# Four conv layers on one core: the planner's freedom on POOL, the queue of the first weights, and the blocks of five weight steps

## The chip, the cores and the metric

The kernel runs on one core of a Trainium2 chip. The metric is the time of one execution in microseconds (us) on the device. The engines are TensorE (PE for the matmuls, PEld for its weight loads), VectorE (DVE), ScalarE (ACT), GpSimd (POOL) and SyncE (SP, which here only starts DMAs). Each runs its own instructions in order and waits for the others by semaphores.

## The reference, cut to what matters

Four layers on x of shape (16, 256, 28, 28). The change lies in what the first layer does and in the weights that the third one needs:

```python
# layer 0
out = sign(x)
scaling = mean(abs(weights), axis=(1, 2, 3))
y = conv3x3(out, sign(weights)) * scaling
yn = (y - mean(y)) * rsqrt(var(y) + EPS)      # over batch and image
x = yn * gamma + beta + x
# layer 1: 3x3 conv of sign(x), gates, 1x1 conv of a sign, residuals
# layer 2: two 3x3 convs of signs with sign(w1), sign(w2), each scaled by mean(abs(w))
# layer 3: attention over the 784 pixels of each image
```

## The kernel before, in words

256 channels are two halves of 128 partitions. A layer with signs on both sides (layer 0 and the two convs of layer 2) is made by `sign_layer` (L273). It packs the weights of two output channels into one number (`dst = 4095 * sign + sign`, L235), so that one matmul makes both halves of the output, and takes them apart again with a rounding trick (`apart`, L298: ACT L302 and L303, DVE L304).

The work goes in 33 blocks of half an image, 392 columns; the last half image is two blocks of 196 (`BLOCKS`, L47). A block is 18 matmuls (`products`, L283; L292): six weight chunks by three taps, into one of three PSUM accumulators (`conv_ps`, L370). Blocks 0 and 1 are made together, chunk by chunk (`together=2`), since at the start the chunks arrive one after the other.

The loop over blocks j (L318 to L333) is written out by hand, in this order: matmuls of block j; ACT's signs of the next image (L398) if j is even; `post` of block j - 1 (statistics on DVE, L532, and for the lower half of an image its store on POOL, L534); at j = 27 `gather` (L153: a memset on POOL, two aggregations on DVE, L157, and L158); `late`, what the last block's step left over; one step; `apart` of block j.

A **step** is a piece of side work, one in each block from j = 2 on; `None` in the list of steps leaves a block without one. In layer 0 (L518 to L527) the list holds seven steps that prepare layer 1's weights (`w1_step`, `fw_step`, here steps 0 to 6), six that prepare the first packed weights of layer 2 (`signs2` and `sums2`, steps 7 to 12), the six sums of layer 0's own absolute weights (`sums_`), and `constants` (L485), which zeroes the two `pad` tiles on POOL (L487), copies to POOL's `doubts`, works out small constants on DVE and starts eight small DMAs. Each of steps 7 to 12 does, through `both` and `sign_weights` (L220): ACT's sign of a 384 KB chunk into tile `sg` (L234; one buffer), DVE's reduction of its absolute values (L246) and the add to the total (L124); left over for the next block is DVE's pack of `sg` (L235), and after the last step `total_up` (L251), four small matmuls on PE (L254) that add the total over partitions. The load of step n + 2 is started on SP after the work of step n (`load_ahead`, L214), into a tile of three buffers.

Who orders the instructions: within `tc.manual_schedule(engines=...)` (L316) those of the named engines that are made in it keep the order of the program among themselves; here PE, ACT, DVE and SP. Everything else is put in order by a planner, which may bring an instruction forward, also into or ahead of such a part. So the memsets of `pad` (L487), made in block 21, ran at 3.89 us.

At the start (L413 to L429) SP starts the DMAs of the first weight chunk, of the first image's two halves, of the other five chunks, and of images 1 and 2; ACT takes the sign of each chunk when it lands. `keep_busy` (L375) gives PE idle matmuls to keep its clock up where it would pause: eight at the start, thirty after layer 0. After layer 0 the statistics are finished (`norm`, L177), image 0 is normalized (`enter`, L587), and layer 1 starts.

Of the kernel before, what the change touches and what calls it, by code (L numbers as in the profile page):

```python
# [35 lines left out]
ET = mybir.EngineType  # L36
# [43 lines left out]
def forward(ctx: ExitStack, tc: tile.TileContext, d: dict, out: bass.AP, careful: bool):  # L80
# [3 lines left out]
    nc = tc.nc  # L84
# [27 lines left out]
    CHUNKS = [(k, g) for g in range(3) for k in range(2)]  # L112
# [10 lines left out]
    def tt(o, a, b, op):  # L123
        V.tensor_tensor(o, a, b, op)  # L124
        return o
# [70 lines left out]
        return r, tt(c, beta, c, ALU.subtract)  # L196


    def load_taps(pool, src, k, g, tag="st", bufs=2):
        st = pool.tile([P, 3, 256], F32, tag=tag, name="st", bufs=bufs)  # L200
        nc.sync.dma_start(out=st, in_=src[k, :, 3 * g:3 * g + 3, :])
        return st

    def packed_weights(pool, **kw):
# [9 lines left out]
    def load_ahead(steps, n, now=True):  # L214

        for s in steps[:n] if now else ():
            s.load()
        return [lambda s=s, t=t: (s.work(), t.load() if t else None)[0] for s, t in zip(steps, steps[n:] + [None] * n)]

    def sign_weights(pool, dst, src, total, acc, stage=("st", 2), tmp=None, ab_tag="rn", sg=("sg", 1)):  # L220


        sts, all_ = {}, []
        tmp = tmp or pool

        def load(k, g):
            if (k, g) not in sts:
                sts[k, g] = load_taps(pool, src, k, g, *stage)

        def sign(k, g):  # L230
            st = sts[k, g]
            n = CHUNKS.index((k, g))
            t = tmp.tile([P, 3, 256], BF16, tag=sg[0], name="sg", bufs=sg[1])
            A.activation(t, st, AF.Sign, saturate=False)  # L234
            return lambda: V.scalar_tensor_tensor(  # L235
                dst[:, n], t[:, :, P:], PACK, t[:, :, 0:P], ALU.mult, ALU.add
            )

        def add_up(k, g):
            st = sts.pop((k, g))  # L240
            if not all_:
                all_.append(tmp.tile([P, 256], F32, tag="total", name="sums", bufs=1))
                ab = all_[0]
            else:
                ab = tmp.tile([P, 256], F32, tag=ab_tag, name="ab", bufs=2)
            V.tensor_reduce(ab, st.rearrange("p t o -> p o t"), AX.X, ALU.add, apply_absolute_value=True)  # L246
            if ab is not all_[0]:
                tt(all_[0], all_[0], ab, ALU.add)
            return total_up if (k, g) == CHUNKS[-1] else lambda: None

        def total_up():  # L251
            part = acc.tile([P, 2], F32, tag="sm", name="sumabs")
            for mo in range(2):
                T.matmul(part[:, mo:mo + 1], lhsT=all_[0][:, mo * P:(mo + 1) * P], rhs=ones, start=True, stop=True)  # L254
            V.tensor_scalar(total, part, 1.0 / K9, None, ALU.mult)

        return [[Step(lambda c=c: load(*c), lambda c=c, f=f: f(*c)) for c in CHUNKS] for f in (sign, add_up)]

    def both(first, second):
        def work(f, s):  # L260
            rest = f.work(), s.work()
            return lambda: [r() for r in rest]

        return [Step(f.load, lambda f=f, s=s: work(f, s)) for f, s in zip(first, second)]
# [8 lines left out]
    def sign_layer(pads, w, temp, room, sign, post, steps, moments, together=1):  # L273

        pss = [None] * NB
        abs_ = [None] * NB

        groups = 2 if careful else 1  # L280
        size = 6 // groups

        def products(*js):  # L283
            for j in js:
                pss[j] = conv_ps()
            for n, (k, g) in enumerate(CHUNKS):
                for j in js:
                    i, r0, rows = BLOCKS[j]
                    for t in range(3):
                        r, c = divmod(3 * g + t, 3)  # L290
                        r += r0
                        T.matmul(  # L292
                            pss[j][:, n // size, :rows * S].rearrange("p (a b) -> p a b", b=S), lhsT=w[:, n, t, :],
                            rhs=pads[:, i % 2, k, r:r + rows, c:c + S],
                            start=(n % size == 0 and t == 0), stop=(n % size == size - 1 and t == 2),
                        )

        def apart(j):  # L298
            for g in range(groups):
                n = BLOCKS[j][2] * S  # L300
                t, ab, ps = temp("t1")[:, :n], room(j, g), pss[j][:, g, :n]
                A.activation(t, ps, AF.Identity, bias=rounding, scale=1.0 / PACK)  # L302
                A.activation(ab[:, 1], t, AF.Identity, bias=unrounding)  # L303
                V.scalar_tensor_tensor(ab[:, 0], ab[:, 1], -PACK, ps, ALU.mult, ALU.add)  # L304
                if g == 0:
                    abs_[j] = ab
                else:
                    tt(abs_[j], abs_[j], ab, ALU.add)

        def sign_image(i):  # L310

            for r0, r1 in ((0, HR + 1), (HR + 1, S)) if i < together else ((0, S),):
                sign(i, slice(r0, r1), lambda k: inner(pads[:, i % 2], k, r0, r1))

        late = None
        with tc.manual_schedule(engines={ET.PE, ET.Activation, ET.DVE, ET.SP}):  # L316
            sign_image(0)
            for j in range(NB):  # L318
                if j == 0:
                    products(*range(together))  # L320
                elif together <= j:
                    products(j)
                if j % 2 == 0 and j // 2 + 1 < B:
                    sign_image(j // 2 + 1)
                if j > 0:
                    post(j - 1, abs_[j - 1])
                if j == EARLY + 1:
                    moments.gather()
                if late:
                    late()  # L330
                step = steps.pop(0) if j >= 2 and steps else None
                late = step() if step else None
                apart(j)  # L333
            post(NB - 1, abs_[NB - 1])
        assert not steps and not late

    def inner(pad, k, r0=0, r1=S):
        return pad[:, k, 1 + r0:1 + r1, 1:S + 1]
# [28 lines left out]
    with tc.tile_pool(name="ps_conv", bufs=3, space=PSUM) as psc, \  # L367
            tc.tile_pool(name="ps_sm", bufs=2, space=PSUM) as pss:

        def conv_ps():  # L370
            return psc.tile([P, 2, 512], F32, tag="cv", name="cv")
# [9 lines left out]
        with tc.tile_pool(name="ph1", bufs=1) as ph:  # L381
# [4 lines left out]
            def load_x(b, integers=False, rows=((0, S),)):  # L386
                if not xs[b]:
                    xs[b] = ph.tile([P, 2, N], F32, tag="xs", name=f"xs{b}", bufs=4)
                for r0, r1 in rows:
                    n = slice(r0 * S, r1 * S)  # L390
                    nc.sync.dma_start(out=xs[b][:, :, n], in_=d["x"][b][:, :, n])
                if integers:
                    ns[b] = ph.tile([P, 2, N], F32, tag="n", name=f"n{b}", bufs=2)
                    nc.sync.dma_start(out=ns[b], in_=n0d[b])
# [7 lines left out]
            def temp(tag):  # L402
                return ph.tile([P, HN], F32, tag=tag, name=tag, bufs=2)
# [9 lines left out]
            signs, sums_ = sign_weights(ph, w0, d["w0"], sf0, pss, ("yu", 6), sg=("t1", 2))  # L413
# [2 lines left out]
            keep_busy(8)  # L416

            top, bottom = ((0, HR + 1),), ((HR + 1, S),)
            signs[0].load()
            load_x(0, rows=top)  # L420
            load_x(0, rows=bottom)
            for step in signs[1:]:
# [39 lines left out]
            def fw_step():  # L462
                sts = []

                def load():
                    sts.append(xpool.tile([P, 3, 256], F32, tag="x2", name="stf", bufs=3))
                    nc.sync.dma_start(out=sts[0][:, 0:2, :], in_=d["fw"])

                return Step(load, lambda: split2(fw, sts[0][:, 0:2, :]))
# [48 lines left out]
            steps = [w1_step(k, c) for k in range(2) for c in range(3)] + [fw_step()]  # L518
            w2a = packed_weights(wpool, tag="wa2")
            signs2, sums2 = sign_weights(xpool, w2a, d["w2a"], sf1, pss, ("x2", 3), tmp=ph)  # L520
            steps = load_ahead(steps + both(signs2, sums2), 2)
# [1 line left out]
            for i, x in enumerate(sums_):  # L523
                steps[3 * i + 1:3 * i + 1] = [x.work, None]
            steps[19:19] = [constants, None]
            steps[-5:-5] = [None]
            steps[-2:-2] = [None]  # L527

            def post0(j, ab):
                b, r0, rows = BLOCKS[j]  # L530
# [4 lines left out]

            mom = block_moments("l0")
            sign_layer(fpads, w0, temp, room0, sign0, post0, steps, mom, together=2)
            for b in range(2):
                xs[b] = None
# [327 lines left out]
            with tc.manual_schedule(engines={ET.PE, ET.DVE, ET.Activation}):  # L867
# [23 lines left out]
                g = gates(hidden_b(B, hidden_a(B, px)))  # L891
# [41 lines left out]
                g = gates(h)[:, 1]  # L933
# [27 lines left out]
        with tc.tile_pool(name="ph2", bufs=1) as ph:  # L961
# [56 lines left out]
            steps = both(*sign_weights(xpool, w2b, d["w2b"], sf2, pss, ("x2", 3), tmp=ph, ab_tag="sums"))  # L1018
# [5 lines left out]
            steps = [first_loads, None] + [t for s in load_ahead(steps, 2, now=False) for t in (None, None, s, None)]  # L1024
# [590 lines left out]
```

## Time and profile before

| | |
|---|---|
| median of 6 runs | 1019.25 us (1018.17 to 1020.11) |
| the profiled execution | 1023.42 us; its span, first to last instruction, 1021.6 us |
| PE busy | 998.7 us, 98% of the span |
| mean granted clock of PE | 0.991 |
| layer 0, first to last matmul of L292 | 7.34 to 126.50 us |
| waits of PE in the first 132 us | 7.1 us, of which 3.0 for the first memset |
| stretches of layer 0 at a granted clock of 0.50 | 9.44 to 16.27 and 122.08 to 128.90 us |

A line of the profile names engine, source line, operation, and the tiles as output<-input; "x18" is a count. In a timeline the first two numbers are start and duration in us, and in brackets stand the idle time of the engine before the instruction and what ended it. In the windows view the columns after the duration are the busy time and the count of each engine, then the clock granted to PE (1.00 is full), the busy share of the DMA engines and GB/s. All times count from the span's first instruction. PE's matmuls overlap, so the time from one start to the next is more telling than the duration.

### The profile page before, as it was taken

The page shows a single profiled execution, that of the slowest core. Times are in us where ns is not written, and L with a number is a line of the kernel's source. Part 1 is how long each engine was busy: PE and PEld are TensorE (multiplying, and loading weights), DVE is VectorE, ACT ScalarE, POOL GpSimd, SP SyncE. Part 2 cuts the span into 40 slices and gives each one's busy share as a digit, 9 for nine tenths or more (in the row PEclk, how much of TensorE's full clock was granted, in tenths as well). Part 3 has the DMA queues.
Part 4 walks back from the last instruction along what each step waited for, and adds up shares of the span by engine and source line. Part 5 has one row for each costly group of instructions (what it writes and reads, how often), then busy time and mean ns, then how long its engine had stood idle before and what let it go on. Part 6 is the DMA issues. An engine that isn't in the chain of part 4 may idle for free.

```text
span 1021.6 us, 14936 instructions
## 1 busy us (share of the span) xinstructions
PE 998.7 (98%) x5663; PEld 825.1 (81%) x5663; DVE 828.1 (81%) x1470; ACT 658.1 (64%) x1103; POOL 140.0 (14%) x149
## 2 busy tenths in 40 slices
PE   7999999999999999999999999999999999999995
PEld 6999889999999999998699998999844444444442
DVE  3888898899999899995689996888856776867765
ACT  6766535656655656654788876777676676666652
POOL 3000100000000000000100000000034444353531
PEclk8999899999999999999999999999999999999998
DMA  9878632222333322110472100000031534334312
GB/s 340 307 272 299 226 126 86 104 95 95 126 127 101 121 95 95 64 64 32 170 302 95 55 9 1 1 2 1 1 63 33 127 69 121 85 106 101 90 64 98
DMA packets 25381, 111.61 MB, mean 109 GB/s; under 512 B 3202, under 2 KB 6980, under 8 KB 25300
## 3 DMA queue, kind: packets, MB, share of 16 engines
q1 hardware_dynamic: 18644, 73.59, 20.1%
q0 software_dynamic: 6656, 36.97, 12.9%
q8 instruction: 47, 0.77, 0.3%
q14 instruction: 34, 0.28, 0.1%
HBM read 72.01 MB, written 38.54 MB: 108 GB/s over the span
## 4 chain that ended last, share of the span: by engine, by line
PE 92%; DVE 4%; ACT 2%; issue 1%; DMA 1%; SPq 0%; DVEq 0%; ACTq 0%
PE cv L626 29%; PE cv L292 29%; PE sc L1202 8%; PE av L1223 8%; PE cv L734 4%; PE mi L1179 4%; PE unused L379 3%; PE sm L1265 2%; PE mi L1283 2%; PE sm L1223 1%; DVE p L1012 1%; PE gate L705 1%; DMA xs<-in_x_dram 1%; PE hid L558 1%; DVE l2b_fin L1013 0%
## 5 line engine op out<-in xcount | busy, mean ns | idle before, releaser
L292 PE MATMUL cv<-fpads,wpk 128*128 128x392 f32 (+1 forms) x1782 | 335.5, 351 | 4.4 <-DVE wpk L235 2.0
L292 PEld LDWEIGHTS cv<-fpads,wpk 128*128 128x128 f32 x1782 | 331.8, 193 | 8.5 <-POOL pad L487 1.6
L626 PE MATMUL cv<-vs,w 128*128 128x392 f32 x1536 | 301.3, 354 | 0.0
L626 PEld LDWEIGHTS cv<-vs,w 128*128 128x128 f32 x1536 | 286.2, 190 | 2.2
L1206 ACT ACTIVATE es<-sc 128x784 f32<-128x784 f32 x112 | 87.4, 822 | 41.6 <-PE sc L1202 41.4
L1202 PE MATMUL sc<-q,keyswa 64*128 64x392 f32 x448 | 89.9, 513 | 0.9 <-ACT es L1206 0.9
L1012 DVE SCALAR_TENSOR_TENSOR p<-ab,vec 128x392 f32<-128x392 f32 (+1 forms) x132 | 79.9, 606 | 2.3
L1223 PE MATMUL av<-es,v 128*64 128x392 f32 x448 | 80.7, 499 | 0.0
L302 ACT ACTIVATE t<-cv,rounding 128x392 f32<-128x392 f32 (+1 forms) x99 | 56.2, 568 | 33.5 <-PE cv L292 30.5
L1202 PEld LDWEIGHTS sc<-q,keyswa 64*128 64x128 f32 x448 | 38.9, 186 | 44.0 <-issue 17.1
L1216 POOL TENSOR_TENSOR sum<-sum,es 128x784 f32<-128x784 f32 x32 | 67.2, 2101 | 3.1 <-ACT es L1206 0.6
L1223 PEld LDWEIGHTS av<-es,v 128*64 128x64 f32 x448 | 29.4, 136 | 47.4 <-issue 47.0
L124 DVE TENSOR_TENSOR vs<-pad 128x840 fp32r<-128x840 bf16 (+1 forms) x66 | 64.4, 1000 | 0.1
L1190 DVE COPY keyswa<-mi 64x392 f32<-64x392 f32 x31 | 16.3, 564 | 52.7 <-ACT q L1186 52.7
L762 POOL DMA_DIRECT2D x2d<-x x16 | 8.6, 537 | 358.9 <-DVE x L756 295.6
L304 DVE SCALAR_TENSOR_TENSOR ab<-ab,cv 128x392 f32<-128x392 f32 (+1 forms) x66 | 36.0, 545 | 25.9 <-ACT ab L303 25.9
L647 ACT ACTIVATE t<-cv,c_bn,s_bn 128x392 f32<-128x392 f32 x32 | 21.7, 678 | 51.6 <-PE cv L626 51.6
L1015 ACT ACTIVATE t<-ab 128x392 f32<-128x392 f32 (+1 forms) x66 | 34.0, 515 | 28.9 <-DVE ab L304 28.9
L734 PE MATMUL cv<-z,fw 128*128 128x392 f32 x256 | 48.8, 341 | 1.0 <-ACT z L726 0.9
L747 ACT ACTIVATE u<-cv,c_bn,s_bn 128x784 f32<-128x784 f32 x30 | 30.1, 1006 | 30.2 <-PE cv L734 30.2
L734 PEld LDWEIGHTS cv<-z,fw 128*128 128x128 f32 x256 | 45.7, 188 | 2.2 <-ACT z L726 2.2
L1179 PE MATMUL mi<-p,wqk 128*128 128x392 f32 x124 | 45.1, 506 | 0.1
(280 smaller groups left out, 1459.0 us busy)
## 6 DMA issues: line engine op xcount, KB each, us to landing
xs<-in_x_dram SPq DMA_DIRECT2D x30, 784.0 KB, 4.8
n0d<-n POOLq DMA_DIRECT2D x16, 784.0 KB, 5.7
n<-n0d SPq DMA_DIRECT2D x16, 784.0 KB, 4.2
x2d<-x POOLq DMA_DIRECT2D x16, 784.0 KB, 3.6
out_dram<-p SPq DMA_DIRECT2D x15, 784.0 KB, 3.8
p<-x2d POOLq DMA_DIRECT2D x14, 784.0 KB, 6.9
p<-x2d SPq DMA_DIRECT2D x13, 784.0 KB, 8.7
st<-in_w_dram SPq DMA_DIRECT2D x12, 384.0 KB, 7.4
```

The source lines that it names most:

```text
L124: V.tensor_tensor(o, a, b, op)
L292: T.matmul(pss[j][:, n // size, :rows * S].rearrange("p (a b) -> p a b", b=S), lhsT=w[:, n, t, :], rhs=pads[:, i % 2, k, r:r + rows, c:c + S],
L302: A.activation(t, ps, AF.Identity, bias=rounding, scale=1.0 / PACK)
L304: V.scalar_tensor_tensor(ab[:, 0], ab[:, 1], -PACK, ps, ALU.mult, ALU.add)
L626: T.matmul(ps.rearrange("p (a b) -> p a b", b=S), lhsT=w[:, k, c, u, mo * P:(mo + 1) * P], rhs=vs[:, b % 2, u, k, :, c:c + S], start=(n == 0),
L734: T.matmul(ps[:, h, :HN], lhsT=w[:, k, mo * P:(mo + 1) * P], rhs=z2[b][:, k, h * HN:(h + 1) * HN], start=(k + i == 0), stop=(k + i == 2),)
L1012: V.scalar_tensor_tensor(p, y, alpha[:, mo:mo + 1], y, ALU.mult, ALU.max)
L1179: T.matmul(ps[:, h, :HN], lhsT=wqk[:, k, :], rhs=x[b][:, k, h * HN:(h + 1) * HN], start=(k == 0), stop=(k == 1))
L1202: T.matmul(ps[:, h, :HN], lhsT=chunk[rows], rhs=qs[b][rows], start=True, stop=True)
L1206: A.activation(e, ps[:, :, :HN], AF.Exp, scale=0.125)
L1216: (V if late else nc.gpsimd).tensor_tensor(sums[b, late], sums[b, late], e, ALU.add)
L1223: T.matmul(ps[64 * h:64 * h + 64, :HN], lhsT=w, rhs=e[:, h, :], start=start, stop=stop)
```

## The change

Three edits. First, POOL joins the engines whose instructions keep the order of the program in `sign_layer`: in layer 0 these are the stores of each image, the memsets and copies of `constants`, and the memset of `gather`; in layer 2 only that of `gather`. Second, the DMA of the first weight chunk is started by ACT, not SP. Third, the two extra empty blocks among steps 7 to 12 go: these steps stood in blocks 23, 25, 26, 27, 29, 30 and now stand in 23, 24, 25, 26, 27, 28; all earlier steps stay where they were, and blocks 29 to 32 hold no step.

```diff
-    def load_taps(pool, src, k, g, tag="st", bufs=2):
+    def load_taps(pool, src, k, g, tag="st", bufs=2, queue=nc.sync):
         st = pool.tile([P, 3, 256], F32, tag=tag, name="st", bufs=bufs)
-        nc.sync.dma_start(out=st, in_=src[k, :, 3 * g:3 * g + 3, :])
+        queue.dma_start(out=st, in_=src[k, :, 3 * g:3 * g + 3, :])
...
-        with tc.manual_schedule(engines={ET.PE, ET.Activation, ET.DVE, ET.SP}):
+        with tc.manual_schedule(engines={ET.PE, ET.Activation, ET.DVE, ET.SP, ET.Pool}):
...
-            signs[0].load()
+            signs[0].load(queue=nc.scalar)
             load_x(0, rows=top)
             load_x(0, rows=bottom)
...
             steps[19:19] = [constants, None]
-            steps[-5:-5] = [None]
-            steps[-2:-2] = [None]
```

The remaining lines only hand the queue through (`load` and `Step`).

## The prediction

> **What bounds the kernel now.** I read the page first (engines, chain), then the waits of TensorE (PE) in the first 132 us, where every edit lies, then the windows view for the granted clock, then the timelines of DVE and ACT around each PE wait.
>
> ```profile
> PE 998.7 (98%) x5663; PEld 825.1 (81%) x5663; DVE 828.1 (81%) x1470; ACT 658.1 (64%) x1103; POOL 140.0 (14%) x149
> ...
> PE 92%; DVE 4%; ACT 2%; issue 1%; DMA 1%; SPq 0%; DVEq 0%; ACTq 0%
> ```
>
> PE is the bound, so an edit counts only where PE waits, where PE runs at a lower clock, or where a stage ends behind other engines. PE's waits in layer 0 (engine line, releaser, us in total, times, longest):
>
> ```profile
> PE unused L379 <- POOL idle L415: 3.0, 1, 3.0
> PE cv L292 <- DVE wpk L235: 2.0, 2, 1.0
> PE sumabs L254 <- DVE sums L124: 1.5, 1, 1.5
> PE cv L292 <- ACT fpads L398: 0.6, 1, 0.6
> ```
>
> Three places: the first microseconds, and one wait of 1.5 us at L254, near the end. Between them PE doesn't stop once: a block's 18 matmuls start 0.1895 us apart, 3.41 us a block. The clock (columns: stretch, us, busy time of PE, PEld, DVE, ACT, POOL, PEclk, DMA):
>
> ```profile
> 9.44:16.27 6.83, 5.84 (x18) 5.64 (x18) 2.79 (x5) 5.76 (x9) 0.00 (x0) 0.50 1.04 404
> 122.08:128.90 6.82, 6.82 (x28) 5.10 (x28) 4.89 (x16) 1.87 (x5) 0.74 (x2) 0.50 0.35 122
> ```
>
> Both times that PE paused, the clock went to 0.50 for 6.83 us. Matmuls of 392 columns are then 0.327 us apart, those of 196 columns 0.213 us, not 0.113. The second stretch follows the wait at L254:
>
> ```profile
> 80.18 0.50 PE L254 MATMUL sumabs<-ones,sums 128*128 128x1 f32 x4
> ...
> 121.75 0.74 PE L254 MATMUL sumabs<-ones,sums 128*128 128x1 f32 x4 [1.47 <-DVE sums L124]
> 122.36 4.14 PE L292 MATMUL cv<-fpads,wpk 128*128 128x196 f32 x18
> ```
>
> So the last half block took 4.14 us where the one before it took 2.15, and PE ended layer 0 at 126.50. At 80.18 the same L254 of layer 0's own sums waited for nothing: DVE had finished the sums at 79.73, 0.45 us before. L254 stands in PE's order between two blocks and waits for the `add_up` of the last step, one block earlier on DVE. What decides is how far DVE is behind there:
>
> ```profile
> 102.55 0.56 DVE L304 SCALAR_TENSOR_TENSOR n<-n,cv 128x392 f32<-128x392 f32 x1 [0.37 <-ACT n L303]
> ...
> 106.80 0.56 DVE L304 SCALAR_TENSOR_TENSOR n<-n,cv 128x392 f32<-128x392 f32 x1 [0.63 <-ACT n L303]
> 107.40 1.04 DVE L532 BATCH_NORM_STATS2 l_fin<-n 128x6 f32<-128x392 f32 x2
> 108.35 1.56 DVE L157 BATCH_NORM_AGGREGATE l_fin<-l_parts 128x2 f32<-128x156 f32 x2
> ...
> 112.62 0.56 DVE L304 SCALAR_TENSOR_TENSOR n<-n,cv 128x392 f32<-128x392 f32 x1 [0.63 <-ACT n L303]
> ```
>
> ```profile
> 104.80 0.84 ACT L234 ACTIVATE sg<-st 128x768 bf16<-128x768 f32 x1 [0.78 <-DVE wpk L235]
> 110.61 0.84 ACT L234 ACTIVATE sg<-st 128x768 bf16<-128x768 f32 x1 [3.84 <-DVE wpk L235]
> ```
>
> These are L304 of blocks 25, 26 and 27. When two steps stand in neighbouring blocks, ACT's sign of the second must wait for DVE's pack of the first, because `sg` has one buffer; and the pack is behind L304 and the statistics. The loop is L304 0.60, statistics 0.95, pack 0.59, sign 0.75, L302 0.61, L303 0.64: 4.14 us (4.25 above, where the pack took 0.66 and not 0.55), against PE's 3.41. Block 27 also holds `gather`: 112.62 - 106.80 = 5.82.
>
> **Part 3, the two blocks.** Now steps 7 to 12 stand at blocks 23, 25, 26, 27, 29, 30; the gaps at 24 and 28 let DVE catch up. After, they stand at 23 to 28 without a gap, and L254 comes in block 29. Each moved step carries a sign (ACT 0.84), a reduction, an add and a pack (DVE 1.03, 0.42, 0.55) and a 384 KB load on SP. L304 of block 23 is at 95.74, set by PE. Then 24: 99.88, 25: 104.02, 26: 108.16, 27: 108.16 + 5.82 = 113.98. In block 28 the sum of step 12 follows: from L304 at 102.55 to the add's end at 106.17 is 3.62, less 0.11 for the slow pack, 3.51: 117.5. PE has finished block 29's matmuls at 114.73. So L254 waits 2.8 us, against 1.47 now, and it is in front of three blocks instead of one. PE has three accumulators, and no L304 here is late enough to hold it earlier (block 29 needs L304 of 26, done at 108.7, and starts at 111.31).
>
> The loads: a step's load goes out when the reduction three steps back is done; here that is at 94.95 for step 10, about 98.8 for 11, about 103 for 12, and they are used from about 106, 110 and 116. Landing took 3.0 to 10.0 us, so none is late. SP's loads of layer 1's images go past them as now. The store of image 14 on POOL follows block 29's statistics, 2.5 us later than now; the reload behind it landed at 127.45 for a use at 130.35, and both move alike.
>
> **Part 1, Pool in program order.** It puts the two 128x1800 memsets (L487) behind the store of image 9, since `constants` stands at block 21. The store went out at 82.52 for 0.53, so they would run at about 83.05 to 86.3. Off the start they free DVE, which they blocked:
>
> ```profile
> 5.50 1.65 DVE L181 TENSOR_SCALAR l_half<-vec 128x2 f32<-128x2 f32 x1 [5.50 <-DMA vec<-in_vecs_dram]
> 5.71 1.45 DVE L235 SCALAR_TENSOR_TENSOR wpk<-sg 128x384 fp32r<-128x384 bf16 x1
> ```
>
> A tensor_scalar of 128x2 took 0.16 elsewhere; here four instructions end at 7.15 to 7.17, just after the second memset's end at 7.10. The pack would end at 6.3. That is hidden: the next group of matmuls waits for the second weight chunk, landed at 9.12, signed by 9.98, packed by 10.57. At the new place DVE's L269 stands at 83.21, 0.16 us behind the memset. Bounds: nothing, if DVE is first; 3.1 us, if both memsets pass; I take one, 1.5 us, since the row shows a wait for one memset. The 1.5 us goes through ACT's L270 and L302 to L304 of block 20 (87.0), through `constants`' short chain to block 21 (91.8); block 22 has no step, so at block 23 it is +0.3 (with 3.1: +1.9). This adds to L254's wait: 3.1 us, not 2.8. `gather`'s memset (0.09) is free, since before it ran ahead of everything, which shows that nothing in its tile orders it.
>
> **Part 2, the first weights on ScalarE's queue.** The image's first DMA goes out at 0.75, not 1.20: 0.45 sooner at most. From 5.75 the DMA engines are full (share 1.04 above), and the second chunk, behind the same bytes, decides: between 0 and 0.45 us. PE is at half clock there, so 0.45 is worth 0.45 x 0.1895 / 0.327 = 0.26. I take 0.2 gained. Were the table load (1.28) first on ACT, chunk one would land at 5.3 and be packed by 6.8, still before 7.34: no loss.
> The page "DMA: Bandwidth & Descriptors" (Issuing engines are not separate DMA queues) says that a second issuer only saves issue time; by it the gain would be issue time alone, which is the same term.
>
> **The sum.** Block 30 starts at 114.73 + 3.1 + 0.61 (L254) = 118.44. At full clock PE ends at 118.44 + 3.41 + 2.04 + 2.15 = 126.0, 0.5 before now. The clock steps lie on a grid of 3.41 us (9.44 and 122.08 are 33 steps apart); the wait fills most of 115.25 to 118.67, so half clock would go from 118.67 to 125.5: one matmul of block 30 at full clock, 17 at 0.327 (124.2), six of block 31 at 0.213 and 12 at 0.113 (126.8), block 32 2.15: 129.0, which is +2.4. With the start: **+2.2** against the profiled execution (span 1021.6, time 1023.42). The grid needn't start with the kernel: in other runs the old wait of 1.47 may be split between two steps and not slow the clock, which would end the old layer up to 1.4 us sooner (L304 of block 31 then sets the end). So +2.2 to +3.6 on the median of 1019.25; I take +2.5: **1021.8**.
>
> The page "TensorE: Matmul & The Clock Gate" (What's actually happening) gives an idle window of about 3.4 us as the condition for the low clock. By it a wait of 2.8 to 3.1 us would not slow PE, and the sum would be the 126.0 above. The row differs: 1.47 us of waiting was enough here.
>
> **Rivals.**
> (a) The clock stays: 126.0, less 0.2: -0.7 against the profile, up to +0.7 against the median: 1019.2. For it: when the clock falls is known from two stretches only. Against: the waits before both of them were shorter than 2.8 us. 20%.
> (b) Both memsets pass DVE: wait 4.7, block 30 at 120.06, end 130.0: +3.3 to +4.7, about 1023.2. 13%.
> (c) Faster: DVE isn't behind at L254. It decides at 114.7: if the sum of step 12 is done by then, PE runs 114.73 + 0.61 + 3.41 + 2.04 + 2.15 = 122.9 at full clock, and the end is 3.6 sooner against the profile, 2.2 against a run without the old half clock: 1015.6 to 1017. For it: the row at 80.18. Against: it needs 2.8 us less between 95.74 and 117.5, and the loop is four measured passes. 15%.
> (d) The change doesn't do what it says: the planner keeps the memsets early, or the queue brings nothing. That takes 0.3 or 0.2 from or to the forecast, so it counts as the forecast, which has 52%, of which about an eighth falls under +2.04.
>
> Measured differences under 0.2% (2.04 us) can't be told from none. Slower: 0.455 + 0.13 = 0.585; same: 0.065 + 0.20 + 0.01 = 0.275; faster: 0.14. The range leaves out most of (c) and the end of (b): 1017.8 to 1024.2.
>
> **What would show it.** PE's wait at L254 near 115 to 118, about 3 us; a stretch at 0.50 behind it; L304 4.1 us apart in blocks 23 to 26; L487 near 83, and L269 longer than 0.41; the first L292 before 7.34. A wait at L254 under 1 us would make the forecast wrong, a long one at full clock would make it (a).

## The result, and the profile after

The changed kernel took 1022.23 us (median of 18 runs, 1020.70 to 1024.38), the kernel before beside it 1019.64 us (38 runs, 1017.82 to 1022.18). The ratio is 1.0024, with a 95% interval of 1.0018 to 1.0031: slower by about 2.5 us. The ratios here and below can differ a little from the quotient of the two medians.

The profiled execution of the changed kernel took 1022.02 us (span 1020.2, mean granted clock 0.994). That is 1.4 us less than the profiled execution before, although the medians stand the other way; how both can be true is told below. First the page: engines, and the chain of work that ended last.

```profile
PE 996.6 (98%) x5663; PEld 823.3 (81%) x5663; DVE 829.5 (81%) x1470; ACT 658.1 (65%) x1103; POOL 140.7 (14%) x149
...
PE 89%; DVE 6%; ACT 2%; issue 1%; DMA 1%; SPq 0%; DVEq 0%; ACTq 0%
```

PE is still the bound, but DVE's share of the chain is 6% where it was 4%: the chain now runs through DVE in front of a wait of PE. The waits of PE in the first 132 us (engine line, releaser, us in total, times, longest):

```profile
PE sumabs L254 <- DVE sums L124: 4.2, 1, 4.2
PE unused L379 <- POOL idle L415: 3.0, 1, 3.0
PE cv L292 <- DVE wpk L235: 0.6, 1, 0.6
```

The wait at L254 grew from 1.5 to 4.2 us, and the waits for the packs at the start fell from 2.0 to 0.6. The timeline of PE around L254, and the windows around it on the grid of the clock's steps (columns: stretch, its us, busy time of PE, PEld, DVE, ACT, POOL, the granted clock, DMA share, GB/s):

```profile
115.52 1.02 PE L254 MATMUL sumabs<-ones,sums 128*128 128x1 f32 x4 [4.20 <-DVE sums L124]
116.39 9.67 PE L292 MATMUL cv<-fpads,wpk 128*128 128x392 f32 x54
```

```profile
107.49:110.90 3.41, 3.41 (x20) 3.40 (x19) 3.34 (x7) 1.08 (x2) 0.00 (x0) 1.00 0.35 144
110.90:114.31 3.41, 0.42 (x3) 0.07 (x1) 2.74 (x6) 2.58 (x5) 1.44 (x3) 1.00 0.15 59
114.31:117.73 3.42, 2.21 (x8) 2.21 (x9) 2.71 (x6) 2.82 (x5) 0.35 (x1) 0.50 1.00 292
117.73:121.14 3.41, 3.41 (x12) 3.41 (x12) 2.14 (x8) 0.00 (x0) 0.62 (x1) 0.50 0.58 240
```

In the second window PE was busy for 0.42 of 3.41 us; the next two run at half clock, 6.83 us as before. Block 30 took 5.66 us there. At the start, in contrast, nothing runs at half clock once the full clock has come:

```profile
8.50:15.30 6.80, 6.16 (x33) 5.82 (x32) 2.79 (x5) 5.94 (x10) 0.00 (x0) 1.00 1.03 400
```

33 matmuls fall in these 6.8 us, where 18 did before. Now DVE, whose lateness is behind L254: L304 of blocks 24, 25, 26 and 27 (left out here: what stands between them).

```profile
97.74 0.56 DVE L304 SCALAR_TENSOR_TENSOR n<-n,cv 128x392 f32<-128x392 f32 x1 [0.63 <-ACT n L303]
...
101.88 0.56 DVE L304 SCALAR_TENSOR_TENSOR n<-n,cv 128x392 f32<-128x392 f32 x1 [0.64 <-ACT n L303]
...
106.01 0.56 DVE L304 SCALAR_TENSOR_TENSOR n<-n,cv 128x392 f32<-128x392 f32 x1 [0.63 <-ACT n L303]
...
111.83 0.56 DVE L304 SCALAR_TENSOR_TENSOR n<-n,cv 128x392 f32<-128x392 f32 x1 [0.63 <-ACT n L303]
```

They stand 4.14, 4.13 and, with `gather`, 5.82 us apart, each time released by ACT's L303, while PE needs 3.41 for a block. And the two memsets (timelines of POOL and of DVE):

```profile
79.53 3.15 POOL L487 MEMSET pad<- 128x1800 bf16 x2
```

```profile
79.65 3.31 DVE L269 TENSOR_SCALAR stf<-stf 128x512 f32<-128x512 f32 x1
```

L269 started 0.12 us after the first memset and ended 0.28 us after the second one; in the kernel before it took 0.41.

Where the difference of the two profiled executions comes from can be summed. Block 19 starts at 73.21 and not at 76.77, 3.56 sooner: 1.16 from the earlier start of PE's long run (9.47 and not 10.63), the other 2.4 from the half clock of 9.44 to 16.27, which this execution didn't have. The wait at L254 gives back 4.20 - 1.47 = 2.73, and L254 itself and the blocks around it 0.39. The half clock behind L254 costs the same in both: the matmuls of blocks 30 to 32 take 9.7 us in either, L254 and its wait not counted. So layer 0 ends 0.44 sooner, at 126.06.

The executions of one kernel differ in this too, and a part of it can be read from the mean granted clock that each run lists. The changed kernel: seven runs at 0.996 took 1020.70 to 1021.78, nine at 0.994 took 1021.78 to 1024.38. The kernel before, in one of the later comparisons: three runs at 0.991 to 0.993 took 1022.44 to 1022.82, the thirteen at 0.996 to 0.998 took 1018.42 to 1021.43. The profiled execution of before, at 0.991, was of the slow end of this spread.

The mean granted clock leaves out one thing, the first microseconds. In the fourteen profiles the record of the clock begins only at 5.98 to 12.13 us (6.02 in the profile before, 8.50 after). Until then PE runs at half pace: the idle matmuls of 512 columns start 0.43 us apart, where those after layer 0 at full clock start 0.22 apart. But the views print 1.00 for a stretch that has no record. So a run can be slow at a high mean clock; among the thirteen fast runs just named, those at 0.998 took 1020.31 to 1021.20.

### The profile page after: what moved, and what is told of

It reads as the page before. It is cut to its first block, busy times and chain, and to the rows that moved or that the text cites. A ratio compares the mean times of both kernels' runs of the same rounds, so it can differ in the third digit from the quotient of the medians.

```text
span 1020.2 us, 14934 instructions
## 1 busy us (share of the span) xinstructions
PE 996.6 (98%) x5663; PEld 823.3 (81%) x5663; DVE 829.5 (81%) x1470; ACT 658.1 (65%) x1103; POOL 140.7 (14%) x149
## 4 chain that ended last, share of the span: by engine, by line
PE 89%; DVE 6%; ACT 2%; issue 1%; DMA 1%; SPq 0%; DVEq 0%; ACTq 0%
PE cv L624 29%; PE cv L292 27%; PE sc L1200 8%; PE av L1221 8%; PE cv L732 4%; PE mi L1177 4%; PE sm L1263 2%; PE unused L379 2%; PE mi L1281 2%; PE sm L1221 1%; DVE p L1010 1%; DVE l_parts L530 1%; PE gate L703 1%; PE hid L556 1%; DMA xs<-in_x_dram 1%
## 5 line engine op out<-in xcount | busy, mean ns | idle before, releaser
L304 DVE SCALAR_TENSOR_TENSOR ab<-ab,cv 128x392 f32<-128x392 f32 (+1 forms) x66 | 36.0, 545 | 25.9 <-ACT ab L303 25.9
```

## The experiments

All were timed in five rounds against the kernel before. In the table, "wait" is PE's wait at the second L254 in the profile. A run of idle matmuls can lack one record in a trace, so that x29 stands below for 30 and x13 for 14.

| kernel | median, us | before beside it | ratio (95% interval) | wait, us |
|---|---|---|---|---|
| the change | 1022.23 | 1019.64 | 1.0024 (1.0018 to 1.0031) | 4.20 |
| e1_pool | 1021.69 | 1019.96 | 1.0014 (1.0005 to 1.0023) | 2.49 |
| e2_queue | 1019.10 | 1019.96 | 0.9993 (0.9984 to 1.0002) | 1.35 |
| e3_steps | 1023.27 | 1019.96 | 1.0024 (1.0012 to 1.0036) | 2.78 |
| e4_pool_queue | 1020.42 | 1019.96 | 1.0000 (0.9991 to 1.0009) | 2.48 |
| e5_awake | 1020.69 | 1020.18 | 1.0006 (0.9995 to 1.0017) | 1.17, behind idle matmuls |
| e6_two_sg | 1019.29 | 1020.18 | 0.9983 (0.9972 to 0.9994) | 2.04 |
| e7_pads_later | 1022.14 | 1020.18 | 1.0015 (1.0003 to 1.0026) | 2.77 |
| e8_total_late | 1019.57 | 1020.18 | 0.9991 (0.9977 to 1.0004) | none |
| f1_total_late_awake | 1017.28 | 1020.67 | 0.9966 (0.9954 to 0.9978) | none |
| f2_total_late_sg | 1016.24 | 1020.67 | 0.9956 (0.9942 to 0.9971) | none |
| f3_steps_total_late_sg | 1016.33 | 1020.67 | 0.9954 (0.9941 to 0.9967) | none |
| f4_before_total_late | 1020.00 | 1020.67 | 0.9990 (0.9979 to 1.0001) | none |

By the ratios the parts alone are worth +1.4 us (Pool's order), -0.7 (the queue; its interval reaches +0.2) and +2.4 (the two blocks). Their sum is 3.1, the whole change 2.5: they add up within the intervals.

**Pool in program order alone** (e1_pool).

```diff
-        with tc.manual_schedule(engines={ET.PE, ET.Activation, ET.DVE, ET.SP}):
+        with tc.manual_schedule(engines={ET.PE, ET.Activation, ET.DVE, ET.SP, ET.Pool}):
```

> Part 1 alone: POOL in program order, the rest as before. Theory (the steps without gaps cause the loss): the memsets L487 run near 83 us and hold L269 for 3.3 us, but the empty blocks 22, 24 and 28 give that back, so L254 waits 1.5 to 1.8 us as before; the first pack is free at 6.2 instead of 7.15 but the second chunk still decides; time -0.5 to +0.3 us. Rival (the memsets behind image 9 cause the loss): +2 to +3 us, with a wait at L254 of about 3 us.

It was slower, ratio 1.0014, and the gaps among the steps didn't absorb the delay. L269 took 3.31 us here too (at 81.92), and ACT's L270 waited 3.42 for it. One more thing came of it, a few blocks on (the timeline of ACT, block 24):

```profile
96.58 0.59 ACT L302 ACTIVATE t<-cv,rounding 128x392 f32<-128x392 f32 x1 [0.38 <-PE cv L292]
...
99.32 0.62 ACT L303 ACTIVATE n<-t,unrounding 128x392 f32<-128x392 f32 x1 [2.15 <-DMA n0d<-n]
...
100.59 0.57 ACT L302 ACTIVATE t<-cv,rounding 128x392 f32<-128x392 f32 x1
```

L303 writes into `n`, which has two buffers, and waits 2.15 us until the store of image 10 has read one of them. DVE was late, so the store went out late, at 92.71, and then ACT was late for the block after. That is how a delay of blocks 20 to 22 outlived block 22, which has no step: counted from the start of block 19, L304 of block 24 is 2.1 us later than in the kernel before, and the wait at L254 is 2.49 and not 1.47.

**The queue alone** (e2_queue). ACT starts the first weight DMA; the rest as before.

```diff
-            signs[0].load()
+            signs[0].load(queue=nc.scalar)
```

> Part 2 alone: the first weight chunk asked for on ScalarE's queue. Theory: the second chunk lands near 8.0 instead of 9.12 us and PE's long run of L292 starts 1.1 us sooner, time -0.6 to -1.2 us. Rival (the sooner start in the changed kernel's profile was the clock's doing alone): the second chunk lands within 0.3 us of 9.12, time within 0.3 us of before.

Ratio 0.9993: a gain of 0.7 us that the interval doesn't quite secure. The profile shows where it is from. PE's long run starts at 9.42, and the second chunk landed at 7.91 where it was 9.12. The windows from 2 to 8 us (stretch, us, busy PE, clock, DMA share, GB/s) show more than an earlier issue (the clock's record begins at 6.90 us here and at 6.02 in the kernel before, so that the 1.00 of the first windows is no reading):

```profile
2.00:6.00 4.00, 3.02 (x8) 1.00 0.98 331
6.00:8.00 2.00, 1.22 (x6) 1.00 1.01 381
```

The same windows of the kernel before:

```profile
2.00:6.00 4.00, 3.02 (x8) 1.00 0.94 261
6.00:8.00 2.00, 1.02 (x5) 1.00 0.92 317
```

At nearly the same busy share the DMA engines moved 331 and not 261 GB/s. Over all profiles: the four kernels without this part moved 257 to 277 GB/s from 2 to 6 us, and their long run began at 9.82 to 10.63; the ten with it 297 to 334, and 9.27 to 10.54.

**The two blocks alone** (e3_steps).

```diff
             steps[19:19] = [constants, None]
-            steps[-5:-5] = [None]
-            steps[-2:-2] = [None]
```

> Part 3 alone: steps 7 to 12 without the two gaps. Theory: L254 waits about 2.8 us in front of block 30 and a stretch at half clock follows; time +2.5 to +3.5 us. Rival (the memsets cause the loss): the wait stays under 3 us but costs no more than the old one, time within 1 us of before.

Ratio 1.0024. The wait at L254 was 2.78 us; L304 of blocks 23 to 26 stood 4.13 to 4.14 apart. But in the profiled execution the clock stayed up behind this wait, and the time went elsewhere (timelines of PE and of DVE):

```profile
115.64 0.61 PE L254 MATMUL sumabs<-ones,sums 128*128 128x1 f32 x4 [2.78 <-DVE sums L124]
116.11 7.66 PE L292 MATMUL cv<-fpads,wpk 128*128 128x392 f32 x54
123.83 6.42 PE L379 MATMUL unused<-idle 128*128 128x512 bf16 x29
134.10 2.28 PE L624 MATMUL cv<-vs,w 128*128 128x392 f32 x8 [3.85 <-DVE vs L124]
```

```profile
130.79 1.03 DVE L588 SCALAR_TENSOR_TENSOR xs<-n,l_r,xs 128x784 f32<-128x784 f32 x1 [3.19 <-DMA n<-n0d]
```

Layer 0 ended at 123.77, but DVE waited 3.19 us for the reload of image 0. It goes into the buffer of `n` that the store of image 14 must have read; that store went out at 119.16, and the reload behind it only at 124.86. (In the whole change the two stood at 119.03 and 122.77, and DVE didn't wait.) The runs of this kernel fall into two groups, five at 1019.92 to 1021.26 and seven at 1023.18 to 1025.28. This profile (1024.40) belongs to the second; that the late reload is what makes the group was not shown for the others.

**Pool's order and the queue, with the gaps kept** (e4_pool_queue).

```diff
-        with tc.manual_schedule(engines={ET.PE, ET.Activation, ET.DVE, ET.SP}):
+        with tc.manual_schedule(engines={ET.PE, ET.Activation, ET.DVE, ET.SP, ET.Pool}):
...
-            signs[0].load()
+            signs[0].load(queue=nc.scalar)
```

> Parts 1 and 2 without part 3: the changed kernel with the two empty blocks back. Theory: L254 waits 1.5 to 1.8 us, PE starts its long run of L292 about 1.1 us sooner; time -1.0 to -1.5 us against before, the fastest of the four. Rival (memsets): +1 to +2 us. Rival (clock's doing): within 0.3 us of before.

Ratio 1.0000: the queue pays for the memsets. The wait at L254 is 2.48, as with Pool's order alone. So the third part is what makes the change slower as a whole.

**PE kept busy in the wait** (e5_awake). To the changed kernel, in front of step 12's L254:

```diff
         def total_up():
             part = acc.tile([P, 2], F32, tag="sm", name="sumabs")
+            if total is sf1:
+                ps = acc.tile([P, 512], F32, tag="sm", name="awake")
+                for _ in range(14):
+                    T.matmul(ps, lhsT=idle[:, 0:P], rhs=idle, start=True, stop=True)
```

> The changed kernel, with 14 idle matmuls of 512 columns put on TensorE directly in front of the second L254. They are done inside the wait for the sums (4.20 us in the profile after; 14 of them take about 3.0 us), so the wait ends when it ended before, but TensorE is not quiet in it. Theory 1 (the half clock behind the wait costs time of its own): the wait of the first matmul of L254 behind the idle ones is about 1 us, block 30 takes 3.4 us and not 5.66, the first matmul of layer 1 is 2.2 us sooner, and the time is 1019.6 to 1020.8, against about 1022.2 for the changed kernel. Theory 2 (the reload of image 0 decides as soon as layer 0 ends sooner): block 30 is also at full clock, but the first pass of layer 1 over image 0 waits for the reload, and the time falls by less than 1 us: 1021.2 to 1022.2.

Ratio 1.0006, 1.8 us under the change. First the timeline of PE, then the windows from 108.60 on, on this run's clock grid:

```profile
113.11 2.97 PE L255 MATMUL awake<-idle 128*128 128x512 bf16 x13
117.25 0.61 PE L258 MATMUL sumabs<-ones,sums 128*128 128x1 f32 x4 [1.17 <-DVE sums L124]
117.72 7.66 PE L296 MATMUL cv<-fpads,wpk 128*128 128x392 f32 x54
```

```profile
112.01:115.43 3.42, 3.35 (x17) 1.89 (x17) 2.72 (x6) 2.99 (x5) 0.93 (x2) 1.00 0.00 0
115.43:118.84 3.41, 2.24 (x14) 1.69 (x12) 2.71 (x5) 2.95 (x5) 0.86 (x2) 1.00 0.99 305
118.84:122.25 3.41, 3.41 (x24) 3.40 (x23) 2.93 (x10) 0.90 (x3) 0.61 (x1) 1.00 0.53 217
```

PE still stands still, as seen by layer 0, for 4.2 us before L254, but blocks 30 to 32 take 7.66 us and not 9.67. That fits theory 1: the half clock behind the wait is worth about 2 us of its own.

**More buffers for the signs** (e6_two_sg). To the changed kernel:

```diff
-            signs2, sums2 = sign_weights(xpool, w2a, d["w2a"], sf1, pss, ("x2", 3), tmp=ph)
+            signs2, sums2 = sign_weights(xpool, w2a, d["w2a"], sf1, pss, ("x2", 3), tmp=ph, sg=("yu", 6))
```

> The changed kernel, but the signs of layer 1's weights go through a ring of six buffers that stands unused at that time, and not through one buffer. A sign on ScalarE need then not wait for VectorE's pack of the step before. Theory 1 (the loop through the one buffer sets VectorE's pace, and that sets the wait at L254): L304 of blocks 24 to 26 stand 3.4 to 3.6 us apart and not 4.14; the wait at L254 is 1.6 to 2.4 us and not 4.2; the time is 1019.6 to 1021.0. Theory 2 (VectorE's own work, not the loop, sets its pace): L304 stays 4.0 us or more apart, the wait over 3.5, the time within 0.8 us of the changed kernel's 1022.2.

Ratio 0.9983, 4.2 us under the change and below the kernel before; more than theory 1 gave it. L304 of blocks 23 to 26 stands at 95.56, 99.33, 102.75 and 106.52, that is 3.4 to 3.8 apart, and no sign waits for a pack. PE (timeline, and the windows from the wait on):

```profile
115.31 0.60 PE L254 MATMUL sumabs<-ones,sums 128*128 128x1 f32 x4 [2.04 <-DVE sums L124]
115.78 9.10 PE L292 MATMUL cv<-fpads,wpk 128*128 128x392 f32 x54
```

```profile
112.82:116.23 3.41, 1.37 (x9) 1.03 (x8) 3.34 (x6) 1.21 (x2) 1.44 (x4) 1.00 0.78 319
116.23:119.64 3.41, 3.41 (x12) 3.41 (x12) 2.87 (x10) 0.00 (x0) 0.61 (x1) 0.50 0.13 55
```

So the loop through `sg` did set DVE's pace. Of the 4.2 us, 2.16 are the shorter wait and about 0.6 the shorter half clock (9.67 - 9.10). The rest isn't in this profile, which is of the slowest of this kernel's runs (1020.78). In the others, most of them at mean clocks of 0.996 and 0.997, the half clock can have been missing; that was not shown.

**The memsets one block later** (e7_pads_later). To the changed kernel:

```diff
-            def constants():
+            def zero_pads():
...
+            def constants():
...
-            steps[19:19] = [constants, None]
+            steps[19:19] = [constants, zero_pads]
```

The new step holds only the two memsets.

> The changed kernel, with the two 128x1800 memsets in a step of their own one block later, where VectorE has no tensor_scalar. Theory 1 (the memsets hold VectorE's L269 and so cost what Pool in program order costs): L269 takes 0.4 us and not 3.31, L304 of block 23 is set by TensorE again, the wait at L254 is about 2.8 us and not 4.2, and the time is 1.4 us under the changed kernel's: 1020.4 to 1021.2. Theory 2 (with the steps two blocks sooner, the end of layer 0 is so late, by the half clock and by the reload of image 0, that 1.4 us less of waiting is lost again): the wait is 2.8 us and the time within 0.7 us of 1022.2, since the two-blocks part alone, which has no memset there, was at 1023.3.

The mechanism is as theory 1 has it (timelines of DVE and of PE):

```profile
82.17 0.41 DVE L269 TENSOR_SCALAR stf<-stf 128x512 f32<-128x512 f32 x1
```

```profile
116.61 0.67 PE L254 MATMUL sumabs<-ones,sums 128*128 128x1 f32 x4 [2.77 <-DVE sums L124]
```

The wait went from 4.20 to 2.77, and L304 of block 23 starts 18.97 us after block 19 does, as in the kernel before; in the change it is 20.40. The time is unclear: the median of 1022.14 is theory 2's, and the ratio of 1.0015 stands 0.9 us under the change's with intervals that overlap. The runs spread by the clock, from 1019.4 at 0.996 (two runs) to 1022.7 to 1023.5 at 0.993 (five), so a wait of 2.77 can cost what one of 4.20 does.

**L254 out of the blocks** (e8_total_late). Pool's order, the queue, the gaps as before, the memsets one block later, and the sum of step 12 called after layer 0:

```diff
-            return total_up if (k, g) == CHUNKS[-1] else lambda: None
+            if (k, g) != CHUNKS[-1]:
+                return lambda: None
+            if last is None:
+                return total_up
+            last.append(total_up)
+            return lambda: None
...
-            keep_busy(30)
+            keep_busy(27)
...
                 tt(mix_c[:, 0], pv("a_scale"), bi0, ALU.mult)
+                total1[0]()
```

> Both the queue and Pool in program order, the gaps kept where the kernel before has them, the two memsets one block later, and the matmuls of layer 1's sum (the second L254) moved out of the blocks, behind the last half block of layer 0, in place of 3 of the 30 idle matmuls there. Theory 1 (the wait at L254, with the half clock behind it, is what all the parts of this change pay for): no wait of TensorE between the first microseconds and the end of layer 0, no half clock at its end, the first matmul of layer 1 at 125 to 127 us, the time 1016.0 to 1018.0, under both kernels. Theory 2 (with layer 0 ending sooner, the store of image 14 and the reload of image 0 behind it decide): the first pass of layer 1 waits for the reload, and the time is 1018.5 to 1020.

Ratio 0.9991, theory 2's time, but for another reason than theory 2's. PE's timeline, and the windows:

```profile
120.68 5.78 PE L384 MATMUL unused<-idle 128*128 128x512 bf16 x26
126.29 0.50 PE L259 MATMUL sumabs<-ones,sums 128*128 128x1 f32 x4
129.94 6.33 PE L633 MATMUL cv<-vs,w 128*128 128x392 f32 x19 [3.15 <-DVE vs L124]
```

```profile
125.63:129.04 3.41, 1.16 (x8) 0.80 (x6) 2.91 (x12) 0.82 (x1) 0.21 (x1) 1.00 0.58 243
129.04:132.45 3.41, 2.51 (x8) 2.54 (x9) 3.30 (x11) 2.06 (x4) 0.00 (x0) 0.50 0.69 221
```

PE ended layer 0 without a wait, ran out of idle matmuls, waited 3.15 us for the first tile of layer 1, and the half clock came there. The reload held DVE only 0.33 us. By the clock, the runs go from 1016.39 and 1016.99 at 0.998 to 1020.92 to 1022.63 at 0.992 (four).

**The same with 38 idle matmuls** (f1_total_late_awake).

```diff
-            keep_busy(27)
+            keep_busy(38)
```

> The kernel e8_total_late with 38 idle matmuls in place of 27 between layer 0 and layer 1. In its profile TensorE waited 3.15 us there for VectorE's first tile of layer 1, and the clock went to 0.50 for 6.83 us from 129.04 on, so that the first 6 us of layer 1's matmuls ran at half speed. Theory 1 (the half clock only moved, from block 30 into layer 1, and took back what the missing wait gave): that wait is under 1.2 us, no stretch at 0.50 between 16 and 1000 us, and the time is 2 to 3 us under that of e8_total_late: 1016.3 to 1017.5. Theory 2 (the end of layer 0's own chain and the reload of image 0 set it, not the clock): the time is within 1 us of 1019.6.

Ratio 0.9966: theory 1. The wait is 1.16 us, no stretch of the profile after 7.86 is at half clock until the end of the kernel, and all six runs, at 0.997 and 0.998, lie within 1016.93 to 1017.86. The spread of the others is gone with the half clock.

**And the ring for the signs** (f2_total_late_sg).

```diff
-tmp=ph, last=(total1 := []))
+tmp=ph, sg=("yu", 6), last=(total1 := []))
...
-            keep_busy(38)
+            keep_busy(36)
```

> As f1_total_late_awake (36 idle matmuls), and the signs of layer 1's weights through the unused ring of six buffers. In e6_two_sg this let VectorE keep up: the wait at L254 fell from 4.20 to 2.04 us, and the time by 2.9 us. Theory 1 (VectorE's lag at the end of layer 0 is what sets the first matmul of layer 1 now): VectorE's last L304 of layer 0 is 1 us nearer to TensorE's last matmul, and the time is 0.7 to 1.5 us under that of f1_total_late_awake. Theory 2 (VectorE has caught up by then through the gaps, and the reload of image 0 decides): no difference, within 0.4 us.

1016.24 us, ratio 0.9956, 1.0 under f1_total_late_awake: theory 1. DVE's last L304 of layer 0 starts 1.0 us after PE's last block ends (120.01 and 119.02), in f1_total_late_awake 2.9 (121.50 and 118.64). PE (timeline):

```profile
119.09 7.72 PE L384 MATMUL unused<-idle 128*128 128x512 bf16 x35
126.64 0.50 PE L259 MATMUL sumabs<-ones,sums 128*128 128x1 f32 x4
127.01 9.32 PE L633 MATMUL cv<-vs,w 128*128 128x392 f32 x48
```

Layer 1's first matmul now waits for nothing: the idle matmuls end last.

**The same without the gaps** (f3_steps_total_late_sg), so with all three parts of the change.

```diff
-            steps[-5:-5] = [None]
-            steps[-2:-2] = [None]
```

> As f2_total_late_sg, but without the two gaps: the steps two blocks sooner, as the change has it. Theory 1 (the only price of the missing gaps was paid at L254, in front of TensorE; without that wait four blocks at the end are free for VectorE to catch up): its last L304 follows TensorE's last matmul by 2.5 us or less, the first matmul of layer 1 is 0.5 to 1.5 us sooner than in f2_total_late_sg, and the time that much lower: 1014.5 to 1016. Theory 2 (the run of steps makes L304 so late that an accumulator or a store is late too, as in the profile of the two-blocks part alone): the time is 1 us or more above f2_total_late_sg.

1016.33 us, ratio 0.9954: neither theory's time, no difference to f2_total_late_sg. DVE's last L304 follows PE's last block by 1.0 us (121.27 and 120.29), as theory 1 has it, but that brought nothing. Here too the first matmul of layer 1 follows L254 without a wait (127.91, 128.27), so a faster DVE has nothing left to give. It shows what the third part costs where PE has no wait for DVE in it: nothing that these runs can tell. The ring is in both, and it alone took the loop through `sg` away in e6_two_sg; so how much of this is due to the ring and how much to the late L254 isn't told. These two are the fastest, 4.5 and 4.7 us under the kernel before.

**The late L254 in the kernel before** (f4_before_total_late), with 38 idle matmuls and nothing of the change.

```diff
-            keep_busy(30)
+            keep_busy(38)
...
+                total1[0]()
```

> The kernel before, with nothing of the change but the same late second L254 and 38 idle matmuls between the layers. It tells whether the gain of f1_total_late_awake needs any of the change. Theory 1 (all of it is the wait at L254 and the half clock around it, and the queue gives 0.5 us on top): 1016.8 to 1018, 0.3 to 0.8 us above f1_total_late_awake. Theory 2 (the queue's earlier start, which also keeps the clock up in the first microseconds in some runs, is the larger part): 1018 to 1019.5.

1020.00 us, ratio 0.9990, above what both theories gave. So the queue and Pool's order with the memsets in a harmless place are worth some 2.5 us in this setting, far more than the queue's 0.7 alone. Its profiled execution (1018.44) is only 1.35 above that of f1_total_late_awake; 1.1 of this is there when layer 0's matmuls end, with the full clock first granted at 11.28 and not 7.86. What makes the other runs slower, up to 1020.29 at a clock of 0.998, stays open. Their mean clock can't tell, since it leaves out the half pace of the first microseconds, as told above.

## Why the prediction was right, and where it was wrong

The number, +2.5 us on the median, is what was measured, +2.5 by the ratio. Two terms behind it were too small, with opposite signs: Part 1 by 1.1 us of waiting, Part 2 by 0.5 (the ratio of the queue alone) to 1.0 us (the start of PE's long run). That they nearly cancel is luck.

- **Part 3** was right. The loop was put at 4.14 us and the block of `gather` at 5.82; measured were 4.14, 4.13 and 5.82. "L254 waits 2.8 us" was 2.78 in e3_steps, which has only this part. e6_two_sg shows that the loop is what the prediction said, ACT's sign waiting for the one buffer.
- **Part 1** is a term that was mis-sized. "I take one, 1.5 us": both memsets passed, L269 took 2.9 us more, and L304 of block 23 was 1.43 late and not 0.3, which is the +1.4 between the waits of 2.78 and 4.20. It was rival (b)'s mechanism, at 4.2 and not its 4.7. The row that the choice was made from, 1.45 to 1.65 us, was of instructions that came in during the second memset, with no third one behind it. And "block 22 has no step" is no cover when the store of an image is late too, as e1_pool shows.
- **Part 2** was mis-sized the other way. "0.45 sooner at most" counted the issue alone; PE's long run began 1.16 sooner in the change's profile, where the DMA engines also moved more bytes in 2 to 6 us. That they did was measured in all ten profiles with the part; why they did was not found. The page "DMA: Bandwidth & Descriptors" (Issuing engines are not separate DMA queues) of the Trainium skill gives issue time as the only saving; the runs here show more.
- **The clock** behind L254 was as predicted, two steps of 3.41 us at 0.50, 114.31 to 121.14. e5_awake puts its price at about 2 us. A wait of 2.78 without it, which is rival (a), was seen in the profile of e3_steps.
- **The sum** was made against the profiled execution, where it said +2.2 and -1.4 was measured, and put on the median, where it held. The profiled execution of before had two half-clock stretches and stood 4 us above its median. The prediction corrected for the stretch behind L254 and took the one at the start for a fixture; the change's own start had none. That the choice of +2.5 within +2.2 to +3.6 met the median so closely was luck too. (A slip of rounding besides: 129.0 less 126.50 is 2.5, not the 2.4 that it wrote.)
- "The reload behind it ... both move alike" held in the change (3.74 us from the store of image 14 to the reload, 3.75 before) and failed in e3_steps: there it took 5.70 us (119.16 to 124.86), and DVE waited 3.19.
- **Rivals (c) and (d)** are out: L254 found DVE behind, the memsets stood at 79.53, and the queue brought its part.

So the change is slower because the second L254, whose only duty is a sum that layer 2 needs, stands between two blocks of matmuls and waits for DVE. What delays DVE there (two blocks less to catch up, two memsets) is paid by PE as a wait, and in many runs again by the half clock. The wait of 4.20 us, e5_awake and e6_two_sg show this for the change; the changed kernel with nothing but its L254 moved was not run, and the two blocks alone also paid by the reload. With L254 where PE has nothing to do, the memsets one block later, six more idle matmuls and the ring, the same three parts are in a kernel that is 4.7 us faster than before. The late L254 and idle matmuls without the change gave 1.0 us (f4_before_total_late, an interval that reaches 1.0001), so the gain isn't L254's alone.

## What to carry to other kernels

A small matmul that waits for a side calculation belongs where TensorE idles anyway, because each delay of the side engine can otherwise be paid twice, as a wait and as the half clock behind it. Where a stage's time depends on the clock, list the stretches at half clock before taking differences: one profiled execution stood 4 us off its median here, and the half clock of its start was worth 2.4 of it. A memset moved to another engine's quiet hour must be checked against the other instructions of that hour, here one TENSOR_SCALAR.

## What the runs showed of the hardware

- **When the clock falls.** In every profile the clock changes on a grid of 3.413 us, whose start differs from run to run. With each window of that grid rated by the share of time that PE was busy: in all fourteen profiles together, up to the last 13 us, the clock fell 16 times, and each time the window before it was busy for 0.61 or less (0.57 in the kernel before, 0.12 after the change). Three windows of 0.51, 0.60 and 0.61 were not followed by half clock, and no window of 0.66 or more was. In the last 13 us of the kernel, not counted so far, six more windows of 0.48 to 0.59 (0.52 in the kernel before, 0.49 after the change) were not followed by half clock either. A window of 0.44 or less at full clock always was. So from 0.48 to 0.61 the share alone doesn't decide. A wait of 1.4 to 1.5 us within one window can lower the clock (the kernel before 0.57, e2_queue 0.60) or not (f4_before_total_late, 1.37 us of waiting, 0.60), and a longer one that is split between two windows may not: the 2.78 us of e3_steps made two, of 0.51 and 0.67. What decides between them stays open. The page "TensorE: Matmul & The Clock Gate" (What's actually happening) of the Trainium skill gives an idle window of about 3.4 us as the condition; the length of the window agrees with the grid, but here PE was busy for up to 0.61 of the window before a fall.
- **Two memsets in a row** on GpSimd (1.6 us each) held a TENSOR_SCALAR of VectorE that started 0.12 us after the first until both were done: 3.31 us and not 0.41, in the change, e1_pool and e4_pool_queue alike. VectorE's instruction did not get its turn between the two.
- **The first DMAs**: at a busy share of 0.9 to 1.0, 257 to 277 GB/s from 2 to 6 us with the first weights on SyncE's queue, 297 to 334 with them on ScalarE's.
